# A two-layer decoder block on one core: the last group's softmax sums by ones on 32 columns, and another order for the last half's projection, layernorm and feed-forward

## The chip, the cores and the metric

One Trainium2 chip, one of its cores. The metric is the device time of one execution in microseconds, the median of several runs. The profile is one separate execution, with a time of its own.

## What is computed

Four sequences of 1024 tokens by 512 features go through a gated self-attention, a cross-attention to a context of 1024 by 384, and a small feed-forward, each after a layernorm and each added to its input. Everything is fp32. Cut to what the change touches (second attention and feed-forward):

```python
q = (layernorm(x) @ Wq + bq)          # 16 heads of 32
k, v = ctx @ Wk + bk, ctx @ Wv + bv
attn = softmax(q k^T / sqrt(32))      # 1024 x 1024 per head
x = x + (attn v) @ Wo + bo
s = layernorm(x) @ Win + bin_         # 512 -> 64
h = relu(s[..., None] * W1 + b1)      # 64 units, 16 hidden values each
x = x + ((h * W2).sum(-1) + b2) @ Wout + bout
```

## The kernel before, in words

`moderate_path` does the whole work; `general_path` follows only if a check of magnitudes (`marks`, then `flag`) fails. The order of every instruction is written out by hand. There are eight items `u`: phase 0 (self-attention) for four sequences, then phase 1 (cross-attention). An item has two halves `hf` of 512 queries, a half has four groups `g` of four heads, and a group has eight steps `kt`, one for each 128 keys.

A step (L659) computes the scores of four heads into two two-bank PSUM tiles `s` (L549), takes the exponential of each on ScalarE into `e` (L554; six buffers, so three steps' worth), and multiplies the previous step's `e` with the values into `av` (L576). The softmax sums are gathered in two ways. In items with `shared` set (phase 0 and the last item), VectorE adds up `e` of the first two heads over the steps (`es`, L562) and TensorE sums the other two by matmuls with a column of ones (`sm`, L584). In the other items VectorE adds up all four heads. When a group is done, `normalize` copies `av` and `sm` to SBUF, `add_up` (L603) sums `es` over partitions by ones, writes the sums to DRAM and reads them back spread over partitions; `divide` (L627) takes the reciprocals, writes these to DRAM and reads each head's row back to its 32 partitions (`recb`); `multiply` (L655) scales `av` into `q`, whose buffer is reused for the attention's output. These parts come steps later, by a list of due times (`after`, `apart`).

Other work is laid between the steps by `run`, which spreads a list of parts with loads over the 32 steps of a half; a `pause` is load without work. `beside` (L867) writes that list. For the last item it holds, for the half before: the projection (`o`, L705, two parts per tile of 128 tokens, with the residual and the statistics), layernorm (`ln`), the way through DRAM to transposed blocks (`xT`, `tr`), the first feed-forward matmul (`s`, L761). The hidden units (`h`, L776: one 128x256 activation on ScalarE and one accumulation `g` on VectorE each, sixteen times, with two buffers `hid`) and the last matmul (`out`, L794) of a half are held over to the next half.

After the last step (L937 to L957) comes the tail: the last `av`, the loads for the last half, the last group's sums through DRAM in three pieces (`soon.pop`) with the held hidden units between, the held outputs, and then the last half's own projection, layernorm, transposes on TensorE (`across`, L304), feed-forward and outputs, and the flag. There PSUM comes in single banks from `bank()`, of which there are two.

DMAs are issued by SP in the order written; each engine works through its own queue in order.

## Time and profile before

| what | value |
|---|---|
| median of 3 runs | 2274.4 us (2273.26 to 2275.88) |
| profiled execution: its time | 2271.7 us |
| its span | 2269.5 us |
| mean granted TensorE clock | 0.991 |
| TensorE busy | 2198.3 us (97%) |
| VectorE busy | 1566.7 us (69%) |
| ScalarE busy | 1237.1 us (55%) |
| last item's scores begin | about 1972 us |
| last exponential ends | 2198.19 us |
| last addition to the output ends | 2262.43 us |
| flag written | 2263.36 us |

Times in the profile count from the start of the span. Busy shares are averages over stages with different limits; the change lies in the last 300 us, so those are read by their own timeline and stretches. In a line of the timeline the first two numbers are start and duration, the bracket gives the idle time of the engine just before and what ended it. In a line of stretches, each engine's busy time and number of instructions are followed by the granted clock, the DMA engines' share and the GB/s they moved.

### The profile page before, as it was taken

The page shows a single profiled execution, that of the slowest core. Times are in us where ns is not written, and L with a number is a line of the kernel's source. Part 1 is how long each engine was busy: PE and PEld are TensorE (multiplying, and loading weights), DVE is VectorE, ACT ScalarE, POOL GpSimd, SP SyncE. Part 2 cuts the span into 40 slices and gives each one's busy share as a digit, 9 for nine tenths or more (in the row PEclk, how much of TensorE's full clock was granted, in tenths as well). Part 3 has the DMA queues.
Part 4 walks back from the last instruction along what each step waited for, and adds up shares of the span by engine and source line. Part 5 has one row for each costly group of instructions (what it writes and reads, how often), then busy time and mean ns, then how long its engine had stood idle before and what let it go on. Part 6 is the DMA issues. An engine that isn't in the chain of part 4 may idle for free.

```text
span 2269.5 us, 52806 instructions
## 1 busy us (share of the span) xinstructions
PE 2198.3 (97%) x22610; PEld 553.9 (24%) x22610; DVE 1566.7 (69%) x2478; ACT 1237.1 (55%) x1485; POOL 148.2 (7%) x146
## 2 busy tenths in 40 slices
PE   6999999999999999999999999999999999999985
PEld 2322222222222222222222222222222222222212
DVE  4469676796757957567685766777687877756555
ACT  0055545555455554555556565666657565667661
POOL 4000020000000000000000000101010100101011
PEclk9999999999999999999999999999999999999997
DMA  4421123021230211212312140313222132212131
GB/s 129 119 78 50 63 95 107 24 83 64 100 105 18 83 64 63 68 44 70 85 59 77 49 118 12 104 48 96 87 60 76 56 79 67 62 48 68 48 91 40
DMA packets 153861, 162.01 MB, mean 71 GB/s; under 512 B 46624, under 2 KB 92320, under 8 KB 152464
## 3 DMA queue, kind: packets, MB, share of 16 engines
q1 hardware_dynamic: 150160, 157.48, 23.1%
q8 instruction: 179, 2.93, 0.5%
q0 software_dynamic: 2144, 0.98, 0.3%
q14 instruction: 66, 0.54, 0.1%
q10 hardware_dynamic: 1312, 0.07, 0.0%
HBM read 115.68 MB, written 42.76 MB: 70 GB/s over the span
## 4 chain that ended last, share of the span: by engine, by line
PE 85%; DVE 6%; ACT 5%; DMA 2%; issue 2%; SPq 0%; DVEq 0%; ACTq 0%
PE f L87 33%; PE s L549 22%; PE av L576 19%; PE sm L584 6%; DVE es L562 4%; ACT e L554 3%; PE sm L606 3%; ACT hid L781 1%; PE f L798 1%; DMA w<-in_attn_Wo 1%; DVE g L787 1%; PE f L766 1%; DVE xT L302 0%; DMA sum_d<-both 0%; PE f L451 0%
## 5 line engine op out<-in xcount | busy, mean ns | idle before, releaser
L554 ACT ACTIVATE e<-s 128x1024 f32<-128x1024 f32 x1024 | 994.0, 1022 | 736.9 <-PE s L549 546.6
L562 DVE TENSOR_TENSOR es<-es,e 128x1024 f32<-128x1024 f32 x528 | 648.4, 1252 | 288.6 <-ACT e L554 287.9
L549 PE MATMUL s<-q,k 32*64 32x512 f32 x8192 | 631.1, 613 | 14.0 <-ACT e L554 12.3
L576 PE MATMUL av<-e,v 128*32 128x512 f32 x4096 | 553.2, 603 | 0.2 <-ACT e L554 0.2
L87 PE MATMUL f<-xT,w 128*32 128x512 f32 x2816 | 331.6, 592 | 0.0
L570 DVE SCALAR_TENSOR_TENSOR eg<-e,sw,eg 128x512 f32<-128x512 f32 x448 | 318.4, 746 | 2.3
L549 PEld LDWEIGHTS s<-q,k 32*64 32x64 f32 x8192 | 137.8, 129 | 477.0 <-ACT e L554 282.9
L87 PE MATMUL f<-w,q 128*32 128x512 f32 x2048 | 243.2, 596 | 0.2 <-DVE res L804 0.2
L560 DVE TENSOR_TENSOR es<-e 128x1024 f32<-128x1024 f32 x88 | 107.7, 1246 | 181.3 <-ACT e L554 175.6
L576 PEld LDWEIGHTS av<-e,v 128*32 128x32 f32 x4096 | 88.5, 108 | 404.0 <-issue 400.2
L87 PEld LDWEIGHTS f<-xT,w 128*32 128x32 f32 x2816 | 93.1, 110 | 210.4 <-issue 203.2
L584 PE MATMUL sm<-e,sw 128*2 128x512 f32 x1024 | 133.3, 592 | 0.0
L727 POOL TENSOR_TENSOR r<-res,bo_bc 128x512 f32<-128x512 f32 x32 | 40.9, 1278 | 1095.7 <-DVE res L719 725.5
L781 ACT ACTIVATE hid<-sT,units 128x256 f32<-128x256 f32 x128 | 74.8, 601 | 66.2 <-DVE sT L268 36.2
L87 PEld LDWEIGHTS f<-w,q 128*32 128x32 f32 x2048 | 67.0, 111 | 156.5 <-issue 149.9
L87 PE MATMUL f<-w,xT 128*32 128x512 f32 x896 | 104.6, 592 | 0.6 <-DVE q L268 0.6
L87 PE MATMUL f<-ctxT,w 128*32 128x512 f32 x768 | 92.3, 592 | 0.0
L87 PE MATMUL f<-w,ctxT 128*32 128x512 f32 x768 | 91.9, 592 | 0.0
L606 PE MATMUL sm<-es,ones 128*1 128x512 f32 x352 | 69.1, 591 | 4.2 <-DVE es L562 3.4
L787 DVE SCALAR_TENSOR_TENSOR g<-hid,units,g 128x256 f32<-128x256 f32 x120 | 57.9, 483 | 13.3 <-ACT hid L781 4.9
L719 DVE TENSOR_TENSOR res<-f,res 128x512 f32<-128x512 f32 x64 | 43.9, 686 | 30.6 <-PE f L87 30.6
L756 POOL TENSOR_TENSOR res<-res,bout_bc 128x512 f32<-128x512 f32 x28 | 59.8, 2143 | 66.0 <-DVE r L287 65.6
(240 smaller groups left out, 1060.1 us busy)
## 6 DMA issues: line engine op xcount, KB each, us to landing
recb<-rec_d SPq DMA_DIRECT2D x256, 64.0 KB
xT<-rows_d SPq DMA_DIRECT2D x60, 256.0 KB
rows_d<-r SPq DMA_DIRECT2D x60, 256.0 KB
w<-in_xattn_Wo SPq DMA_DIRECT2D x9, 1024.0 KB
xin<-in_x SPq DMA_DIRECT2D x8, 1024.0 KB
w<-wout_d SPq DMA_DIRECT2D x8, 1024.0 KB
res<-in_x SPq DMA_DIRECT2D x32, 256.0 KB
x1b_d<-r SPq DMA_DIRECT2D x32, 256.0 KB
```

Of the source, the lines that this page charges most:

```text
L87: nc.tensor.matmul(to[r], lhsT=lhsT[:, j, :] if len(lhsT.shape) == 3 else lhsT[:, r], rhs=rhs, **flags)
L549: nc.tensor.matmul(s[m : m + 64, j, :], lhsT=k[r, g, kt * P + m : kt * P + m + 64], rhs=q[r, g, :], start=True, stop=True,)
L554: nc.scalar.activation(e, s, AF.Exp, scale=SCALE)
L560: nc.vector.tensor_tensor(me["es"][i], me["e", 0][i], es[i], ALU.add)
L562: nc.vector.tensor_tensor(me["es"][i], me["es"][i], es[i], ALU.add)
L570: nc.vector.scalar_tensor_tensor(eg, es[0][:, h, :], gate(kt), eg, ALU.mult, ALU.add)
L576: nc.tensor.matmul(av[r, :], lhsT=me["v"][:, kt, HG * g + h, :], rhs=es[h // 2][:, h % 2, :], start=(kt == 0), stop=(kt == NT - 1),)
L584: nc.tensor.matmul(sm[j * DH : j * DH + sums, :], lhsT=me["sw"][:, t, HG * g + 2 + h, :] if ph == 0 else ones, rhs=me["e", t][1][:, h, :], ...
L606: nc.tensor.matmul(sm[j * DH : j * DH + 1, :], lhsT=ones, rhs=e, start=True, stop=True)
L756: return lambda: nc.gpsimd.tensor_tensor(res[t], res[t], bout_bc, ALU.add)
L781: nc.scalar.activation(hid, res["s"], AF.Relu, bias=units[:, 1, h : h + 1], scale=units[:, 0, h : h + 1])
L787: nc.vector.scalar_tensor_tensor(res["g"], res["hid"], units[:, 2, h - 1 : h], res["g"], ALU.mult, ALU.add)
```

## The change

The loop. In the last group of the last half (`closing`), VectorE adds up all four heads, TensorE's `sm` matmuls and `normalize` are left out. `beside` for the last item puts the weights and residuals first, spreads the first six held hidden units over pauses, lays the others between the projection's parts, puts the held outputs after the projection, and spreads the first eight of the new hidden units over the end of the half. The second half also fetches the tail's weights and residuals inside the loop.

The tail. `settle` multiplies each head's `es` with ones on 32 columns, so that the sums arrive on all 32 partitions of that head; reciprocal and product are taken for 128 tokens at a time, straight from PSUM. A tile's projection is split into chunks 0 to 2 and chunk 3, the only one that needs the last group. Tiles 2 and 3 project into the score banks (`behind`). Layernorm is done for two tiles at a time, with tiles 1 and 3 normalised on ScalarE; the output bias comes from a matmul with `share` (1/64) into the output's banks; inputs are computed for two tiles at a time; the flag stands ahead of most hidden units.

The diff, without a few renamings (`n`, `rs`):

```diff
@@ -105,6 +105,8 @@
         nc.gpsimd.memset(ones, 1.0)
+        share = const.tile([P, 1], F32, name="share")
+        nc.gpsimd.memset(share, 1.0 / M)
@@ -536,7 +539,12 @@
             shared = ph == 0 or u + 1 == len(order)
-            apart = 2 if u + 1 < len(order) else 3
+            def apart(g):
+                return 2 if u + 1 < len(order) else 3
+            def closing(g):
+                return (u, hf, g) == (len(order) - 1, 1, HG - 1)
@@ -554,7 +562,7 @@
                 me["e", kt] = es
-                for i in range(1 if shared else 2):
+                for i in range(1 if shared and not closing(g) else 2):
                     if kt == 1:
@@ -577,7 +585,7 @@
                     )
-                if shared and kt % 2:
+                if shared and kt % 2 and not closing(g):
@@ -622,7 +630,7 @@
                         )
-                after(apart, lambda: divide(g, i, both, c))
+                after(apart(g), lambda: divide(g, i, both, c))
@@ -650,7 +658,7 @@
                     )
-                after(apart, lambda: multiply(g, both, all_))
+                after(apart(g), lambda: multiply(g, both, all_))
@@ -669,7 +677,7 @@
                 times(g, kt, es)
-                if kt == NT - 1:
+                if kt == NT - 1 and not closing(g):
                     normalize(g)
@@ -677,6 +685,29 @@
+        def settle(u, hf, g):
+            me = S[u]
+            i = (u * 2 + hf) * HG + g
+            rec = p1.tile([P, HALF], F32, tag="recb", name="recb")
+            def sums():
+                for j in range(HG):
+                    nc.tensor.matmul(
+                        sm[j * DH : (j + 1) * DH, :], lhsT=ones.to_broadcast([P, DH]), rhs=me["es"][j // 2][:, j % 2, :],
+                        start=True, stop=True,
+                    )
+            def divide(t):
+                nc.vector.reciprocal(rec[:, ts(t, P)], sm[:, ts(t, P)])
+                nc.vector.tensor_tensor(me["q", hf][:, g, ts(t, P)], av[:, ts(t, P)], rec[:, ts(t, P)], ALU.mult)
+            def look():
+                nc.vector.tensor_reduce(marks[:, i : i + 1], sm, AX.X, ALU.add)
+                nc.vector.tensor_reduce(marks[:, NS + i : NS + i + 1], rec, AX.X, ALU.add)
+            return sums, divide, look
         def post(u, hf):
@@ -686,7 +717,7 @@
                 def f():
-                    if not last:
+                    if (u, hf) not in ((n - 2, 1), (n - 1, 1)):
                         r = res[t] = p4.tile([P, D], F32, tag="res", name="res")
@@ -703,11 +734,14 @@
             def project(t):
-                def part(cs):
+                def part(cs, to=None):
                     def f():
-                        assert me["divided", hf] == HG - 1
+                        assert me["divided", hf] >= cs[-1]
                         if cs[0] == 0:
-                            res["po"] = bank()
+                            res["po"] = to() if to else bank()
+                            res["po", t] = res["po"]
+                        if last:
+                            res["po"] = res["po", t]
                         for c in cs:
@@ -727,24 +761,43 @@
                     return len(cs), f
+                if last:
+                    return [part([0, 1, 2], behind if t > 1 else None), part([3])]
                 return [part([0, 1]), part([2, 3])]
-            def root():
+            def behind():
+                if not res.get("banks"):
+                    two = ps.tile([P, 2, HALF], F32, tag="s", name="s")
+                    res["banks"] = [two[:, i, :] for i in range(2)]
+                return res["banks"].pop(0)
+            def root(a=0, n=4):
                 if ph == 1:
-                    i = 2 * NS + b * NT + 4 * hf
-                    nc.gpsimd.tensor_copy(marks[:, i : i + 4], res["mv"][:, :, 1])
-                res["rs"] = rsqrt(res["mv"], 4)
+                    i = 2 * NS + b * NT + 4 * hf + a
+                    nc.gpsimd.tensor_copy(marks[:, i : i + n], res["mv"][:, a : a + n, 1])
+                rs = rsqrt(res["mv"][:, a : a + n, :], n)
+                for t in range(n):
+                    res["rs", a + t] = rs[:, t : t + 1]
+                if last:
+                    res["nm", a] = p2.tile([P, n], F32, tag="ve", name="nm")
+                    nc.vector.scalar_tensor_tensor(res["nm", a], res["mv"][:, a : a + n, 0], -1.0, rs, ALU.mult, ALU.mult)
...
                             res["xn"] = p1.tile([P, 4, D], F32, tag="tok", name="xn")
-                        normalized(res["xn"][:, t, :], res[t], res["mv"], res["rs"], t)
-                        nc.gpsimd.tensor_tensor(res[t], res[t], bout_bc, ALU.add)
+                        to = res["xn"][:, t, :]
+                        if t % 2:
+                            nc.scalar.activation(
+                                to, res[t], AF.Identity, bias=res["nm", t - 1][:, 1:2], scale=res["rs", t]
+                            )
+                        else:
+                            normalized(to, res[t], res["mv"], res["rs", t], t)
                         return
                     r2 = p2.tile([P, 1, D], F32, tag="r2", name="r2")
-                    normalized(r2[:, 0, :], res[t], res["mv"], res["rs"], t)
+                    normalized(r2[:, 0, :], res[t], res["mv"], res["rs", t], t)
                     away(rows_d[b][hf], r2, t, 1)
@@ -756,18 +809,25 @@
             def tr(t):
-                return lambda: (across if last else blocks)(res["xn"], t)
-            def inputs():
-                ss = bank()
+                def f():
+                    crossing[:] = [True] * (t != 2)
+                    across(res["xn"], t)
+                return f if last else lambda: blocks(res["xn"], t)
+            def inputs(ks=(0, 1)):
+                if 0 in ks:
+                    res["ss"] = bank()
+                ss = res["ss"]
                 for c in range(NC):
-                    for j in range(4):
+                    for j in range(2 * ks[0], 2 * ks[-1] + 2):
                         k, m = divmod(j, 2)
...
                         )
+                if 1 not in ks:
+                    return
                 sT = p2.tile([P, 2 * P], F32, tag="sT", name="sT", bufs=1)
@@ -793,11 +853,11 @@
                 def f():
-                    po = [bank(), bank()]
+                    po = res["bout", t] if last else [bank(), bank()]
                     for k in range(2):
...
                             po[k], lhsT=res["g"][k * M : (k + 1) * M, ts(t, P)], rhs=wout[k * M : (k + 1) * M, :],
-                            start=True, stop=True,
+                            start=not last, stop=True,
                         )
@@ -806,20 +866,32 @@
+            def bout(t):
+                def f():
+                    po = res["bout", t] = [behind(), behind()]
+                    for k in range(2):
+                        r = slice(k * M, (k + 1) * M)
+                        nc.tensor.matmul(
+                            po[k], lhsT=share[r].to_broadcast([M, P]), rhs=bout_bc[r, :], start=True, stop=False
+                        )
+                return f
             loads = [[(0, load(t)) for t in range(4)]]
...
                 "o": [project(t) for t in range(4)],
-                "ln": [[(0, root)]] + [norm(t) for t in range(4)],
+                "ln": ([[(0, lambda a=a: root(a, 2))] for a in (0, 2)] if last else [[(0, root)]])
+                + [norm(t) for t in range(4)],
             }
...
                 "xT": [] if last else [[(0, load_xT)]],
-                "b": [] if last else [[(0, biased(t))] for t in range(4)],
+                "b": [[(2, bout(t))] for t in range(2)] if last else [[(0, biased(t))] for t in range(4)],
                 "tr": [[(1 if last else 0, tr(t))] for t in range(4)],
-                "s": [[(2, inputs)]],
+                "s": [[(2, inputs)]] if not last else [[(1, lambda k=k: inputs((k,)))] for k in range(2)],
                 "h": [[(0, hidden(h))] for h in range(INNER + 1)],
@@ -869,13 +942,15 @@
             if u + 1 == n:
-                out = last["wo"] + end(pause(14)) + last["load"] + pause(2) + last["o"] + weave(last["ln"], pause(8))
-                out += last["xT"] + pause(10) + last["tr"] + weave(last["b"], pause(4)) + last["s"]
-                if hf == 0:
-                    out += pause(5)
-                else:
-                    out += weave(last["h"][0:6], pause(6))
-                    last["h"] = last["h"][6:]
+                h, out = held[0]["h"], last["wo"] + last["load"]
+                k = min(len(h), 6)
+                if hf:
+                    ending.append(post(u, 1))
+                    out += ending[0]["wo"]
+                out += weave(h[0:k], pause(12)) + weave(h[k:], last["o"]) + held.pop()["out"]
+                out += (ending[0]["load"] if hf else []) + weave(last["ln"], pause(5)) + last["xT"] + pause(8)
+                out += last["tr"] + weave(last["b"], pause(2)) + last["s"] + weave(last["h"][0:8], pause(14))
+                last["h"] = last["h"][8:]
                 held.append(last)
@@ -934,27 +1009,38 @@
                 run(attention(u, hf), beside(u, hf))
+        tail = ending[0]
+        sums, divide, look = settle(n - 1, 1, HG - 1)
         late.pop(0)()
-        crossing.clear()
-        tail, before = post(n - 1, 1), held.pop()
-        parts = lambda *names: sum((sum(tail[k], []) for k in names), [])
-        hidden = sum(before["h"], [])
-        run([lambda: None], [parts("wo", "load")])
-        soon.pop(0)[-1]()
-        run([lambda: None], [hidden[0:6]])
-        soon.pop(0)[-1]()
-        run([lambda: None], [hidden[6:]])
-        soon.pop(0)[-1]()
-        run([lambda: None], [sum(before["out"], []), parts("o", "ln", "xT", "b", "tr", "s", "h", "out")])
+        def go(*parts):
+            for _, f in parts:
+                f()
+        o, ln, b, tr, s = ([part for item in tail[k] for part in item] for k in ("o", "ln", "b", "tr", "s"))
+        h = [part for item in held[0]["h"] for part in item]
+        go(o[0])
+        sums()
+        go(o[2], *h[0:3])
+        for t in range(4):
+            divide(t)
+            go(*h[3 + 2 * t : 5 + 2 * t])
+        S[n - 1]["divided", 1] = HG - 1
+        go(o[1], o[3], *o[4:6], *sum(held[0]["out"], []), ln[0], *ln[2:4], *o[6:8], b[0], *tr[0:2], s[0])
+        go(ln[1], *ln[4:6], b[1], *tr[2:4], s[1])
+        look()
         fine = p1.tile([P, 2 * NS + B * NT], F32, name="fine")
...
         nc.tensor.matmul(pn[0:1, 0:1], lhsT=least, rhs=ones, start=True, stop=True)
+        h = sum(tail["h"], [])
+        go(*h[0:4])
         nc.vector.tensor_scalar(flag, pn[0:1, 0:1], P - 0.5, None, ALU.is_lt)
+        go(*h[4:], *sum(tail["out"], []))
```

More of the change, by code (lines that the diff above doesn't have):

```diff
@@ L286, in normalized @@
         def normalized(to, xt, mv, rs, i):
-            nc.vector.tensor_scalar(to, xt, mv[:, i, 0:1], rs[:, i : i + 1], ALU.subtract, ALU.mult)
+            nc.vector.tensor_scalar(to, xt, mv[:, i, 0:1], rs, ALU.subtract, ALU.mult)
         def away(rows, xt, t, n):
@@ L320, in moderate_path @@
         order = [(ph, b) for ph in range(2) for b in range(B)]
+        n = len(order)
         late = []
@@ L385, in f @@
                         xt = me["xn", hf][:, t, :]
-                        normalized(xt, xt, res["mv"], res["rs"], t)
+                        normalized(xt, xt, res["mv"], res["rs"][:, t : t + 1], t)
                         if xt0(hf):
@@ L859, in one @@
             return [[(0, f)]]
+        ending = []
         held = []
```

## The prediction

> **What bounds the kernel now.** I read the page first (busy shares, chain), then the timeline of the last batch item, the groups by shape, the stretches of the tail, and the chain in order of time.
>
> ```profile
> PE 2198.3 (97%) x22610; PEld 553.9 (24%) x22610; DVE 1566.7 (69%) x2478; ACT 1237.1 (55%) x1485; POOL 148.2 (7%) x146
> PE 85%; DVE 6%; ACT 5%; DMA 2%; issue 2%; SPq 0%; DVEq 0%; ACTq 0%
> ```
>
> TensorE bounds the whole. The change touches only the last item (u=7, from 1972 us) and what follows its attention, and there the limits are others. Timeline of that item (start, duration, engine, work, idle before):
>
> ```profile
> 2099.37 1.13 ACT L781 ACTIVATE hid<-sT,units 128x256 f32<-128x256 f32 x2 [0.35 <-DVE g L787]
> 2100.41 1.92 ACT L554 ACTIVATE e<-s 128x1024 f32<-128x1024 f32 x2
> 2101.46 2.00 PE L549 MATMUL s<-q,k 32*64 32x512 f32 x16
> ...
> 2157.15 1.11 PE L549 MATMUL s<-q,k 32*64 32x512 f32 x16
> 2159.38 2.00 PE L549 MATMUL s<-q,k 32*64 32x512 f32 x16
> ```
>
> A step's 16 score records take 1.06 us when both halves of the scores may be written, 2.00 when the second waits for the exponentials. The score starts 2157.15, 2163.17, 2169.19 give 6.02 us for two plain steps; 2011.84 to 2020.21 gives 8.37 for two with a projection part each (1.72), where TensorE is full; 2097.68 to 2104.72 gives 7.04 for two into which ScalarE has to fit five of the feed-forward's 128x256 activations.
>
> The tail, by stretches (us; busy time and count of PE, weight loads, DVE, ACT, POOL; clock; DMA):
>
> ```profile
> 2198.20:2216.49 18.29, 7.72 (x27) 1.92 (x25) 9.71 (x23) 8.44 (x15) 0.00 (x0) 0.72 0.14 45
> 2216.49:2232.20 15.71, 15.67 (x128) 4.09 (x128) 5.32 (x10) 0.00 (x0) 0.00 (x0) 0.89 0.10 35
> 2236.28:2245.50 9.22, 8.02 (x160) 5.90 (x160) 6.41 (x8) 0.00 (x0) 5.50 (x4) 0.81 0.01 2
> 2245.50:2256.04 10.54, 0.00 (x0) 0.00 (x1) 8.10 (x17) 9.36 (x16) 0.00 (x0) 0.75 0.00 1
> 2263.40:2269.50 6.10, 0.00 (x0) 0.00 (x0) 0.00 (x0) 0.00 (x0) 0.00 (x0) 0.50 0.16 51
> ```
>
> and as the chain has it:
>
> ```profile
> 2204.85 2.03 DMA cs<-sum_d
> ...
> 2210.18 1.99 DMA recb<-rec_d
> 2212.28 0.30 DVE q L656
> ...
> 2216.49 15.72 PE f L87 x128
> ...
> 2261.74 0.69 DVE res L804
> ```
>
> Call Z the end of the last exponential: 2198.19. Then nothing overlaps: the sums go through DRAM until Z+14.8, the held outputs until Z+18.3, the projection until Z+34.0, layernorm and transposes until sT at Z+47.3, hidden units until Z+57.9, the last addition at Z+64.2, the flag, the end at Z+71.3.
>
> **The change: the last item's steps.** Work in the loop is moved, not removed, but for 16 `sm` matmuls of the last group (4 x 0.86 = 3.4 us of PE).
>
> First half (1972.08 to 2083.51, 111.4 us). Steps 1-6 now carry one activation each. It fits ScalarE's wait of about 1.8 us in one step of a pair and costs some 0.2 over the 0.29 in the other: 3 pairs x 6.1, plus 0.3 for the copies of the first step, 18.6. Eight steps with a projection part, 4 x 8.37 plus 0.8 for the sums' matmuls between (2036.96 to 2041.53 is 4.57 against 3.76), 34.3; eleven activations lie in these steps' ScalarE waits (1.8 and 2.7 us in each pair). Two steps with outputs, 2 x (1.04+1.00+1.06)+0.86 = 7.1. Sixteen plain steps 48.2; the `win` matmuls, moved to the end of a group, 1.7 and activations again 0.7. Sum 110.6: gain 0.8.
>
> Second half (2083.51 to Z, 114.7). The same 18.8+34.3+7.1, then 24.1 for the third group. Last group: its first step with `win` 5.5 (as 2183.51 to 2189.03); then without `sm` a step is scores 1.06 and values 1.00, against ScalarE's 1.92+0.5: about 2.5 each, 19.0 to Z. Sum 108.8: gain 5.9. Both gains 6.7; from 3 (the activations hidden less well) to 9.
>
> VectorE pays: 14 additions of 1024 columns instead of 7, 1.15 each back to back (four in 4.62 at 1959.84), 7 `g` updates at 0.45, the third group's division and multiplication 1.4: 16.1+3.2+1.4 = 20.7 from the first exponential's end, 2.2 us into a group whose Z comes after 19.0. So the last addition ends near Z+3.6. Six `e` buffers, three steps, cover that lag; without them it would be ScalarE's.
>
> SP now issues the next weights (1 MB), residuals (1 MB) and in the second half another 1 MB at the half's start, ahead of the previous group's bounce. The DMAs moved 383 GB/s at 2194 to 2196, so 3 MB are 8 us; the division is asked for in the fifth step, 12 us in. Hidden; uncovered it would stop VectorE, then PE's first projection part.
>
> **The tail.** From Z on VectorE's order sets the pace; PE's first three projection chunks for two token tiles and the sums (o[0], o[2], 6 us) run beside it.
>
> - Additions end at Z+3.6; four `g` at 0.585 (16 activations in 9.36): Z+5.9. The sums on 32 columns, 1.04 as `sm` before, start at Z+3.6: hidden.
> - Four reciprocals 128x128, four products, six `g`. No such reciprocal is in the trace; two neighbours are:
>
> ```profile
> L643 DVE RECIPROCAL rec<-den 128x16 f32<-128x16 f32 x32 | 8.1, 253 | 1.1
> L477 DVE RECIPROCAL sw<-f 128x64 f32<-128x64 f32 x8 | 4.4, 550 | 0.0
> L787 DVE SCALAR_TENSOR_TENSOR g<-hid,units,g 128x256 f32<-128x256 f32 x120 | 57.9, 483 | 13.3 <-ACT hid L781 4.9
> ```
>
> 48 columns cost 0.297, 6.2 ns each; 128 give 0.95. [...] The second neighbour reads PSUM as well: I take 0.95. Product 0.29 by the same copies, gaps 0.04: 4 x 1.32 + 6 x 0.57 = 8.7, Z+14.6. This takes the place of 4.5+4.8 us of bounce.
> - Three tiles' addition, statistics, aggregate (0.73+0.73+0.20): Z+19.6; PE has them ready from Z+8 to Z+14. Four held outputs, 2.8 and 1.6 of waiting for banks (as 2214.2 to 2215.7): Z+23.9. The root for two tiles is as long as for four, 2.4, and `nm` 0.2; a normalisation 0.55 (1.02 before, with POOL beside it): Z+27.0.
> - Fourth tile: PE starts it when the held outputs have left, Z+21.7. Its 3.44 us become 5.2, since the clock was 0.50 from 2216.5 to 2220 after a like pause: Z+27.1. Then 1.7+2.6+0.55: Z+31.9.
> - Its transposes, 1.1, copy 0.75, 1.1, copy 0.65, half the inputs 1.2: sT at Z+36.7 (before Z+47.3).
> - Hidden units as before, 10.5: Z+47.2. All four output matmuls at once, 2.1 and 1.8, then two additions, 1.4: Z+52.5; the bias is in PSUM, the two bias pairs hidden in PE's waits; the check of `marks` lies before the hidden units.
> - The end came 6.1 us after the flag, 7.1 after the last addition; I take 6.5: Z+59.0.
>
> Gain 71.3-59.0 = 12.3. [...] After Z+14 PE has only short bursts. [...]
>
> Sum: 6.7+12.3 = 19.0. Span 2269.5 to 2250.5; that execution's time 2271.7 to 2252.7; the median of the runs stands 2.7 above it, so 2255.4.
>
> **Rivals.**
> 1. As worked out: 2255.4, own range 2250 to 2260; chance 0.70.
> 2. The loop gives nothing: the spread activations and VectorE's doubled additions hold up the exponentials as much as the clumps did. For it: an activation waits for the `g` two before, now queued behind long additions. Against: 1.8 us of ScalarE wait. Tail alone: 2262.1; 0.14.
> 3. [...] 2261.4; 0.10.
> 4. Slower: the bounce of the previous half's last group, behind the 3 MB. PE, in order, stands at the projection part of each half's eighth step until the product is there. The steps leave 9 us to each leg where 4.5 and 4.8 were needed. To eat 19 us, and 4.5 for a visible loss, both halves' bounces must be some 12 us later than their slots, transfers at a third of the rate seen. 2280; 0.03.
> 5. It does nothing: PE waits for all four products before any projection, and the loop gains nothing. Against: the first three chunks read none of them, and 8.6 us of idle PE before L798 are there to be filled. 2274; 0.03.
>
> **The numbers.** Below 2250 only if the loop gives 9 and the clock holds. 2249 to 2262.5 leaves out rivals 4 and 5 and some of each edge of the others, about 0.2. Measurement tells about 0.2%, 4.5 us: faster 0.94, same 0.03, slower 0.03.
>
> **What would show it.** Projection matmuls right after the last `av`, no DMA between sums and product; score starts 6.0 to 6.2 apart for pairs in steps 1-6 of both halves; Z near 2191.5; the last addition to `es` 3 to 4 us after Z; reciprocals of 0.95; sT at Z+37; the last addition at Z+52. Wrong: a DMA stall of VectorE in the first eight steps, reciprocals over 1.2, a fourth tile projected after Z+30.

## The result

The changed kernel takes 2256.25 us, median of 4 runs (2255.34 to 2258.3), the kernel before 2275.14 in the runs beside them: a ratio of 0.9915, 95% interval 0.9903 to 0.9928, or 18.9 us less (16.4 to 22.1). A second measurement gave 2253.74 and 0.9906 (0.9891 to 0.9921). The profiled execution took 2255.34, its span 2253.5. Forecast were 2255.4 and 19.0 us.

From the page of the changed kernel, busy time by engine (with its share of the span) and the shares of the chain that ended last:

```profile
PE 2192.8 (97%) x22590; PEld 552.6 (25%) x22590; DVE 1572.1 (70%) x2498; ACT 1238.2 (55%) x1488; POOL 142.9 (6%) x144
PE 84%; DVE 7%; ACT 4%; DMA 2%; issue 2%; SPq 0%; DVEq 0%; ACTq 0%
```

As before, the whole says nothing of the change; it lies in the last item and behind. Its timeline, in the first steps of the first half and the last two before Z, the end of the last exponential (now 2194.14):

```profile
1986.54 1.34 PE L557 MATMUL s<-q,k 32*64 32x512 f32 x16
1986.62 0.60 ACT L841 ACTIVATE hid<-sT,units 128x256 f32<-128x256 f32 x1
...
1987.69 1.94 ACT L562 ACTIVATE e<-s 128x1024 f32<-128x1024 f32 x2 [0.47 <-PE s L557]
...
1988.80 1.97 PE L557 MATMUL s<-q,k 32*64 32x512 f32 x16
...
1989.52 0.60 ACT L841 ACTIVATE hid<-sT,units 128x256 f32<-128x256 f32 x1
...
2188.40 1.39 PE L557 MATMUL s<-q,k 32*64 32x512 f32 x16
...
2189.05 0.60 ACT L841 ACTIVATE hid<-sT,units 128x256 f32<-128x256 f32 x1 [0.40 <-DVE g L847]
2189.56 1.94 ACT L562 ACTIVATE e<-s 128x1024 f32<-128x1024 f32 x2
...
2190.72 1.92 PE L557 MATMUL s<-q,k 32*64 32x512 f32 x16
```

One activation stands in each step, and ScalarE still waits (0.47) in every second one of the first steps. In the last group, exponential plus activation, 1.94 + 0.60 and short gaps, make up the step of 2.64 on average. From the item's first score to Z it takes 216.49 us where it took 226.11.

The tail in stretches (columns as before: busy time and count of PE, weight loads, DVE, ACT, POOL; clock; DMA):

```profile
2194.14:2207.08 12.94, 12.27 (x110) 4.38 (x108) 12.14 (x23) 5.30 (x10) 0.00 (x0) 1.00 0.00 1
2207.08:2215.00 7.92, 5.14 (x16) 1.47 (x16) 6.26 (x13) 0.00 (x0) 0.19 (x1) 0.86 0.18 66
2222.80:2225.90 3.10, 3.04 (x24) 1.27 (x28) 1.00 (x5) 0.83 (x2) 0.00 (x0) 1.00 0.00 0
2231.60:2242.20 10.60, 0.00 (x0) 0.00 (x0) 7.72 (x17) 9.70 (x17) 0.00 (x0) 0.74 0.01 2
2242.20:2246.20 4.00, 3.79 (x8) 1.19 (x8) 1.41 (x4) 0.00 (x0) 0.00 (x0) 0.50 0.09 30
2247.40:2253.50 6.10, 0.00 (x0) 0.00 (x0) 0.00 (x0) 0.00 (x0) 0.00 (x0) 0.50 0.26 94
```

In the first stretch TensorE and VectorE are now both nearly full, 12.27 and 12.14 of 12.94 us; in the stretch of the bounce before, they were busy for 7.72 and 9.71 of 18.29. The chain in order of time (start, duration, what) shows who set the end, VectorE up to the held outputs and TensorE from there to sT (the copy that the tail's hidden units start from):

```profile
2203.71 0.88 DVE recb L702
...
2211.58 0.68 DVE res L864
...
2214.98 4.18 PE s L87 x32
2219.16 1.06 PE s L875 x4
...
2222.86 1.92 PE f L824 x16
2224.79 1.06 PE s L875 x4
```

The tail from Z takes 59.36 where it took 71.31. So the parts that the change touches gave 9.62 + 11.95 = 21.6 us in the profiles, where the medians have 18.9 (16.4 to 22.1). The difference is the start, which the change doesn't touch: this execution began its last item at 1977.65, that of before at 1972.08. These 5.6 us arose at three places. The first scores came at 113.3 instead of 111.1. One step of the second group took 1.8 longer, on a clock of 0.80 instead of 1.00 (first line before, second changed):

```profile
166.16:173.08 6.92, 5.68 (x52) 1.30 (x48) 6.85 (x11) 2.96 (x3) 0.00 (x0) 1.00 0.14 38
168.30:177.02 8.72, 7.32 (x53) 1.47 (x49) 8.65 (x14) 2.96 (x3) 0.00 (x0) 0.80 0.11 30
```

One step of the 47th group took 1.7 longer, by just as much as VectorE waited longer for the DMA of `recb` (7.94 instead of 6.22):

```profile
1647.14 0.69 DVE L656 TENSOR_TENSOR q<-both,recb 128x512 f32<-128x512 f32 x1 [6.22 <-DMA recb<-rec_d]
1652.72 0.69 DVE L664 TENSOR_TENSOR q<-both,recb 128x512 f32<-128x512 f32 x1 [7.94 <-DMA recb<-rec_d]
```

Everything else together comes to 0.1 us. The other profiles differ at the same places and at one more, the third step of the first item, near 118 us: 5.50 at a clock of 1.00 in these two, 8.3 to 8.6 at 0.59 to 0.60 in seven others. In all fourteen profiles of this study the last item starts between 1972.08 and 1981.20, and the one of before is the earliest: it had a clock of 1.00 in both steps and the shortest wait for that DMA. So what follows compares parts: the item's first score to Z, and Z to the end. The medians carry a spread that no edit made.

### The profile page after: what moved, and what is told of

It reads as the page before. It is cut to its first block, busy times and chain, and to the rows that moved or that the text cites. A ratio compares the mean times of both kernels' runs of the same rounds, so it can differ in the third digit from the quotient of the medians.

```text
span 2253.5 us, 52768 instructions
## 1 busy us (share of the span) xinstructions
PE 2192.8 (97%) x22590; PEld 552.6 (25%) x22590; DVE 1572.1 (70%) x2498; ACT 1238.2 (55%) x1488; POOL 142.9 (6%) x144
## 4 chain that ended last, share of the span: by engine, by line
PE 84%; DVE 7%; ACT 4%; DMA 2%; issue 2%; SPq 0%; DVEq 0%; ACTq 0%
PE f L87 32%; PE s L557 22%; PE av L584 18%; PE sm L592 6%; DVE es L570 4%; ACT e L562 3%; PE sm L614 3%; DVE g L847 1%; DMA w<-in_attn_Wo 1%; ACT hid L841 1%; PE f L858 1%; PE f L824 1%; DMA rec_d<-rec 0%; DVE xT L304 0%; DMA wae<-in_attn_Wa 0%
## 5 line engine op out<-in xcount | busy, mean ns | idle before, releaser
L87 PE MATMUL f<-w,q 128*32 128x512 f32 x1984 | 238.1, 592 | 0.7 <-DVE q L703 0.7
L664 DVE TENSOR_TENSOR q<-both,recb 128x512 f32<-128x512 f32 x63 | 46.3, 735 | 27.9 <-DMA recb<-rec_d 27.8
```

What stands on the lines that cost most here:

```text
L87: nc.tensor.matmul(to[r], lhsT=lhsT[:, j, :] if len(lhsT.shape) == 3 else lhsT[:, r], rhs=rhs, **flags)
```

## The experiments

The table has, in us, the last item's first score to Z, the tail behind Z, their sum, and where several rounds ran the median and the ratio to before with its interval. A ratio is to the runs of before beside that kernel, whose median was 2274.0 to 2275.7, so it is not the quotient of the medians shown. A row without one is a single execution.

| kernel | loop | tail | sum | median | ratio |
|---|---|---|---|---|---|
| before | 226.11 | 71.31 | 297.42 | 2275.14 | |
| changed | 216.49 | 59.36 | 275.85 | 2256.25 | 0.9915 (0.9903 to 0.9928) |
| changed, again | 216.50 | 59.15 | 275.65 | 2253.74 | 0.9906 (0.9891 to 0.9921) |
| new list alone | 218.72 | 71.71 | 290.43 | 2270.42 | 0.9964 (0.9950 to 0.9978) |
| new tail, old list | 225.84 | 60.06 | 285.90 | 2266.32 | 0.9946 (0.9929 to 0.9964) |
| ones on 32 columns alone | 226.99 | 72.67 | 299.66 | 2276.84 | 1.0001 (0.9989 to 1.0013) |
| changed, bounce back | 218.72 | 64.90 | 283.62 | 2264.20 | 0.9936 (0.9911 to 0.9960) |
| late bias pairs | 216.50 | 58.76 | 275.26 | | |
| the same, five idle matmuls | 216.50 | 57.70 | 274.20 | | |
| fewer additions | 216.18 | 58.74 | 274.92 | | |
| whole tiles | 216.66 | 60.43 | 277.09 | | |
| held additions off VectorE | 216.84 | 56.22 | 273.06 | | |
| four tiles first | 216.52 | 59.55 | 276.07 | 2255.58 | 0.9921 (0.9908 to 0.9935) |
| all three edits | 216.52 | 54.67 | 271.19 | 2251.80 | 0.9887 (0.9869 to 0.9904) |

### Which part brings what

**The new list alone** (the `else` of the old list goes with it):

```diff
-                out = last["wo"] + end(pause(14)) + last["load"] + pause(2) + last["o"] + weave(last["ln"], pause(8))
+                h, out = held[0]["h"], last["wo"] + last["load"]
+                k = min(len(h), 6)
+                out += weave(h[0:k], pause(12)) + weave(h[k:], last["o"]) + held.pop()["out"]
+                out += weave(last["ln"], pause(5)) + last["xT"] + pause(8)
...
```

> The kernel before with one part of the change alone: the new list of work beside the last item's two halves (activations spread over the first steps, projection parts from the seventh step on, residuals loaded early). The last group still takes 16 sm matmuls and the bounce, and the tail is the old one. Theory (the list itself helps, as read from the two traces): steps 1 to 6 of each half shrink as in the changed kernel, so from the item's first score to Z 2.9 + 6.7 us less, minus some 2.3 for the last group that keeps its sm matmuls: 7 to 8 us less than 226.1, tail 71 as before, median 7 us lower. Rival (the gain in the loop comes from the last group and from the shift at the start, the list gives nothing): 226 to Z, median within 3 us of before.

Loop 7.4 us shorter, tail as before: the theory. The median is 5.3 lower than that of before beside it, where 7 was expected. The rival, that the list gives nothing, is out: the ratio's interval (5 to 11 us) excludes the 3 us that it allowed.

**The new tail with the old list:**

```diff
-                h, out = held[0]["h"], last["wo"] + last["load"]
+                out = last["wo"] + end(pause(14)) + last["load"] + pause(2) + last["o"] + weave(last["ln"], pause(8))
...
+                    out += weave(last["h"][0:6], pause(6))
```

> The changed kernel with the old list of work beside the last item, so the tail and the last group are new and the loop is old. Theory: tail 59.4 as in the changed kernel (12 us below before), last group 24.4 (2.3 below), the rest of the loop as before; median 14 us below before, 5 us above the changed kernel; the two experiments together then give back the whole. Rival (list and tail depend on each other: with the old list the hidden units and held outputs come at another time and the tail grows): tail of 62 us or more.

The tail is what was expected within 0.7, so the rival is out; in the two parts the gain is 11.5, not 14. But the last group did not get 2.3 us shorter by losing its `sm` matmuls: 26.48, against 26.77 before and 24.43 in the changed kernel. Up to its last step it had gained 2.6, and the last step gave 2.3 of that back: 5.4 us where it took 3.1 before. The timeline there shows why:

```profile
2194.61 1.91 PE L824 MATMUL f<-xn,win 128*32 128x256 f32 x32
...
2199.43 1.09 ACT L841 ACTIVATE hid<-sT,units 128x256 f32<-128x256 f32 x2
...
2201.77 2.35 DVE L570 TENSOR_TENSOR es<-es,e 128x1024 f32<-128x1024 f32 x2
...
2204.04 1.07 DVE L847 SCALAR_TENSOR_TENSOR g<-hid,units,g 128x256 f32<-128x256 f32 x2
2204.61 0.60 ACT L841 ACTIVATE hid<-sT,units 128x256 f32<-128x256 f32 x1 [1.78 <-DVE g L847]
```

In the old list the activations come in a clump in the last three steps. With two buffers `hid`, the fourth has to wait for `g`, and `g` stands on VectorE behind the additions to `es`, which the change has doubled. ScalarE stands for 1.78, and the last exponential, next in its queue, with it. That is the mechanism of the prediction's second rival, an activation behind long additions, and in the old order of work it is there. In the new list the activations are spread evenly, and these waits are 0.2 to 0.4. (The line of TensorE is for later: the inputs whole, 32 records in 1.91.) In the new list with `sm` kept the same group takes 26.65: there TensorE fills it, busy for 26.3. Either edit alone gives 0.1 to 0.3, both give 2.3. So 7.4 + 0.3 fall short of the 9.6 of the loop by just this.

**Ones on 32 columns alone**, the rest of the tail in the old order:

```diff
-                for i in range(1 if shared else 2):
+                for i in range(1 if shared and not closing(g) else 2):
...
-        soon.pop(0)[-1]()
-        run([lambda: None], [hidden[0:6]])
...
+        sums()
+        run([lambda: None], [hidden[0:3]])
+        for t in range(4):
+            divide(t)
+            run([lambda: None], [hidden[3 + 2 * t : 5 + 2 * t]])
```

> The kernel before with only the last group's sums changed: no sm matmuls in it, both es buffers filled by VectorE, the sums on 32 columns, reciprocal and product in four pieces, no DMA; all of the tail behind it in the old order (the projection starts when all four products are there, the flag last). Theory: the loop 2.3 us shorter in the last group; the products end at Z + 13 to 14.5 where the bounce ended at Z + 14.8, so alone the new division brings at most 2 us in the tail: median 2 to 5 us lower, nearly all of it from the loop. Rival (the bounce was what cost, and its removal is most of the tail's 12 us): median 10 us or more lower.

Less than the theory allowed: nothing at all, the interval being 0.9989 to 1.0013. The products are complete at Z + 12.0 instead of Z + 14.8, but `g`, which finished during the bounce, now alternates with the reciprocals on VectorE until Z + 13.0; the old order has the held outputs next, and those end at Z + 19.4 (18.9 before). The last group keeps 26.5 for the reason just told. And 1.2 of this execution's loop is another matter, a stretch in the second half's third and fourth step where the clock fell in full work:

```profile
2098.72:2100.40 1.68, 1.68 (x12) 0.36 (x12) 0.76 (x2) 1.68 (x3) 0.00 (x0) 0.52 0.07 17
2100.40:2102.30 1.90, 1.90 (x17) 0.20 (x9) 1.77 (x3) 1.55 (x3) 0.00 (x0) 0.53 0.07 7
```

Without that it is some 1.1 us worse than before in these parts, all in the tail. That is partly the held outputs' 0.5 and partly a clock of 0.69 instead of 0.81 under the transposes; the rest was not followed further.

**The changed kernel with the bounce back:**

```diff
-                return (u, hf, g) == (len(order) - 1, 1, HG - 1)
+                return False
...
-        sums()
-        go(o[2], *h[0:3])
-        for t in range(4):
-            divide(t)
-            go(*h[3 + 2 * t : 5 + 2 * t])
+        soon.pop(0)[-1]()
+        go(o[2], *h[0:3])
+        soon.pop(0)[-1]()
+        go(*h[3:])
+        soon.pop(0)[-1]()
```

> The changed kernel with the old division of the last group: 16 sm matmuls, the sums through DRAM, three stages; the new order of projection, layernorm and feed-forward stays. Theory: last group 2.3 us longer; the products at Z + 14.8 instead of Z + 12.9, and with VectorE free during the bounce the held outputs can't go earlier, as they stand behind the products in its order: tail 2 us longer. Median 4 to 5 us above the changed kernel. Rival (VectorE's additions in the last group are the price of the new division, so the old one costs less than the sum): 0 to 2 us above. Rival (the bounce collides with the early residual and weight loads): 8 us or more above.

The loop is the 2.2 longer, the tail 5.5 instead of 2. The step missed: the bounce hands over all 512 columns at once, and TensorE stands until then.

```profile
2214.30 0.69 DVE L664 TENSOR_TENSOR q<-both,recb 128x512 f32<-128x512 f32 x1 [1.38 <-DMA recb<-rec_d]
2215.05 1.93 PE L87 MATMUL f<-w,q 128*32 128x512 f32 x8 [8.73 <-DVE q L664]
```

In the changed kernel the first tile's last chunk runs after a quarter of the division (Z + 6.4), and the third tile is projected at Z + 13.1, just as VectorE gets free of the divisions (Z + 12.9). With the bounce they come after Z + 15.8, at a clock of 0.50 after 8.73 us of standing (8 records in 1.93 where they took 1.07), and the third tile's statistics end at Z + 25.2 instead of 17.5. So the same division is worth 7.8 us in loop and tail of the new order and nothing in the old.

### What sets the tail's pace

**Fewer additions:**

```diff
-                for i in range(1 if shared and not closing(g) else 2):
+                for i in range(1 if (shared and not closing(g)) or (closing(g) and 1 < kt < 7) else 2):
```

> The changed kernel without five of the seven additions to the second es in the last group (key tiles 2 to 6): so it leaves out part of the sums of two of the four heads, and with them 5 x 1.18 = 5.9 us of VectorE. Theory (VectorE is 3.0 us behind at Z, and its order sets the tail's pace): additions end near Z + 1.2, the first reciprocal starts at Z + 3.3 instead of Z + 5.1, and everything to the end comes 1.8 us earlier, Z + 57.6; in the loop the last group stays at 24.4, as ScalarE sets it. Rival (TensorE sets the pace from the projection on): first reciprocal earlier, end within 0.5 of Z + 59.4. Rival (VectorE holds up ScalarE in the last group): group of 22.5 or less.

Nearest to the first rival, just outside its 0.5: the first reciprocal starts at Z + 4.6 (3.3 by the theory), the end comes 0.6 us earlier. The last group is 0.3 shorter, so the second rival (22.5 or less) is out. With its lag gone, VectorE waits for the sums instead:

```profile
2196.95 0.96 DVE L702 RECIPROCAL recb<-sm 128x128 f32<-128x128 f32 x1 [0.91 <-PE sm L696]
```

TensorE takes the sums after `o[0]` and among the first of `o[2]`, up to Z + 4.5; the lag of 3 us costs less than 1, since TensorE's own work covers the rest.

**Whole tiles:** the last group's chunk first in each tile, no chunk ahead of its product.

```diff
-        go(o[0])
         sums()
-        go(o[2], *h[0:3])
+        go(*h[0:3])
...
-                        for c in cs:
+                        for k in cs:
+                            c = (k + 3) % NC if (u, hf) == (n - 1, 1) else k
```

> The changed kernel with the tail's projection taken tile by tile, the last group's chunk first, so that no projection matmul runs before the product of its own tile. Times from Z. Theory (VectorE's order sets the pace; TensorE has slack of 5 us and more): the first tile's 3.44 us start after the first product, Z + 6.4, at half clock for a while, so the three tiles are ready near Z + 11.5, 15 and 18.5 where VectorE asks for them at 12.9, 14.4 and 15.9: its three additions end 1.5 to 2.5 later, and the end comes at Z + 60.5 to 62. Rival (the early chunks are what the tail's gain comes from): the end at Z + 65 or later.

Three tiles at Z + 20.4 instead of 17.5, the end 1.07 later: the theory's end, from a delay of 2.9 where it said 1.5 to 2.5. Part comes back because TensorE, busy until then, did the fourth tile in 3.64 where the changed kernel took 4.25. The early chunks are worth 1 us, not the gain.

**Late bias pairs:**

```diff
-        go(..., *o[6:8], b[0], *tr[0:2], s[0])
-        go(ln[1], *ln[4:6], b[1], *tr[2:4], s[1])
+        go(..., *o[6:8], *tr[0:2], s[0])
+        go(ln[1], *ln[4:6], *tr[2:4], s[1])
...
-        go(*h[0:4])
+        go(b[0], b[1], *h[0:4])
```

> The changed kernel with both bias pairs issued behind the check of marks, among the tail's hidden units, instead of ahead of the transposes. Times are from Z, the end of the last exponential, in the profile. Theory (the second pair stands on TensorE's path between the first half of the inputs and the transposes of the third tile, 1.06 us, and the first pair pushes the transposes of the first tile by 0.99, and with them the first half of the inputs): sT at Z + 35.6 instead of Z + 37.4, end at Z + 57.5 instead of Z + 59.4. Rival (VectorE's second root sets the transposes of the third tile, the pairs are hidden as forecast): end within 0.3 of Z + 59.4.

The end came 0.6 earlier, between the two forecasts, but in this execution the fourth tile's projection, ahead of every edit, took 5.47 instead of 4.25:

```profile
2214.11 5.47 PE L87 MATMUL s<-w,q 128*32 128x512 f32 x32
...
2219.40 1.92 PE L311 MATMUL f<-ident,xn 128*32 128x128 f32 x64
```

From the end of that projection to the end of the span it is 32.52 where the changed kernel has 34.34: 1.82 less, as the theory had it. The pairs were on the path.

**The same with five idle matmuls:**

```diff
         go(b[0], b[1], *h[0:4])
+        for _ in range(5):
+            nc.tensor.matmul(av, lhsT=ident, rhs=bout_bc, start=True, stop=True)
```

> As the run with the late bias pairs, and five 128x512 matmuls more that nobody reads, written into the spent av bank while ScalarE and VectorE work on the tail's hidden units; they add work and take none away. They are to keep TensorE busy, 8 us or so of the 10.7, up to the output matmuls, which took 2.18 us to the first pair at a granted clock of 0.50. Theory (the idle stretch halves the clock, and a busy one restores it): the first pair in 1.1 us, the four additions without a gap, end 1.1 to 1.5 us earlier than with the late pairs alone. Rival (the clock stays down for short work, or the matmuls come to stand ahead of the outputs): 0, or up to 1 us later.

The end came 1.06 earlier than with the late pairs alone, near the forecast, but by luck: 0.86 of it is the fourth tile's projection (4.61 instead of 5.47), ahead of the edit. From sT on it is 0.2, not the 1.1 to 1.5. The five took 4.56 us, not 8, and left TensorE idle for 4.35 before the outputs, which ran at a clock of 0.57 (2.18 to the first pair). Ten were tried later.

**Held additions off VectorE:**

```diff
-                        nc.vector.tensor_tensor(res[i], po[k], res[i], ALU.add)
+                        if (u, hf) == (n - 1, 0):
+                            r2 = p2.tile([P, D], F32, tag="r2", name="r2")
+                            nc.scalar.copy(r2, po[k])
+                            nc.gpsimd.tensor_tensor(res[i], r2, res[i], ALU.add)
+                        else:
+                            nc.vector.tensor_tensor(res[i], po[k], res[i], ALU.add)
```

> The changed kernel with the four additions of the held outputs taken off VectorE in the tail: ScalarE copies them out of PSUM, GpSimd adds. Theory (VectorE's order sets the pace; these additions and their waits take 4.1 us of it between the third tile and the first root): first root at Z + 17.5 instead of Z + 21.6; but the fourth tile's projection still has to follow the output matmuls and its banks, so norm(2) moves less, 1.5 to 3 us, and the end to between Z + 56.4 and Z + 57.9. Rival (GpSimd's additions slow VectorE's small operations beside them, as the normalisation with GpSimd beside it took 1.02 against 0.54): less than 1 us, or later.

3.1 us earlier, as the theory had it at best. The rival's mechanism is there as well, but not its end, less than 1 us. The timeline at the root:

```profile
2214.32 3.80 POOL L867 TENSOR_TENSOR res<-r,res 128x512 f32<-128x512 f32 x3 [0.23 <-ACT r L866]
...
2214.72 0.91 DVE L276 TENSOR_SCALAR ve<-fmv 128x2 f32<-128x2 f32 x1
...
2215.28 3.64 PE L87 MATMUL s<-w,q 128*32 128x512 f32 x32
...
2215.65 1.23 DVE L278 TENSOR_SCALAR yi<-ve 128x2 int32<-128x2 int32 x1
...
2216.92 1.22 DVE L279 TENSOR_SCALAR yi<-yi 128x2 int32<-128x2 int32 x1
...
2218.17 0.16 DVE L283 SCALAR_TENSOR_TENSOR nw<-yi 128x2 f32<-128x2 f32 x1
```

Three operations on two columns, 0.17 each elsewhere, take 0.91 to 1.23 beside GpSimd's additions of 1.27 each, and 0.16 again once those are done: 2.9 us lost. Each of the three took 0.7 to 1.0 times as long as one such addition; why was not shown. What is gained in spite of it: the root starts 4.1 earlier, and the fourth tile follows at once on a clock of 1.00.

### Versions meant to beat it

**Four tiles first:**

```diff
-        go(o[1], o[3], *o[4:6], *sum(held[0]["out"], []), ln[0], *ln[2:4], *o[6:8], b[0], *tr[0:2], s[0])
-        go(ln[1], *ln[4:6], b[1], *tr[2:4], s[1])
+        go(o[1], o[3], *o[4:8], *sum(held[0]["out"], []), *ln)
+        go(*sum(held[0]["held"], []), *tr[0:2], s[0], *tr[2:4], s[1])
...
+        for _ in range(10):
```

> A version meant to beat the changed kernel: in the tail all four tiles are projected and added before the held outputs, one root serves all four; the held outputs are copied out of PSUM by ScalarE and added by VectorE after the normalisations; both bias pairs and ten 128x512 matmuls that nobody reads stand among the hidden units, the latter for the clock. Expected from Z: VectorE's four tiles end at Z + 19.0, root and nm at Z + 21.6, norm(2) at Z + 22.8 (29.8 in the changed kernel), then transposes and inputs in 9 us: sT at Z + 31.5 (37.4), first output pair at full clock, end at Z + 52 (59.4), 7 us less than the changed kernel. Rival (TensorE, cold again before the transposes, or the held outputs' banks hold up the transposes): sT at Z + 34 or later, gain of 4 us or less.

No gain: sT at Z + 38.6. The rival's side, by a wait that neither named:

```profile
2203.77 3.62 PE L87 MATMUL s<-w,q 128*32 128x512 f32 x32
2210.87 5.33 PE L87 MATMUL s<-w,q 128*32 128x512 f32 x32 [3.48 <-DVE res L753]
```

The fourth tile's bank is the second half of one two-bank tile whose first half the third tile uses; its matmuls waited until VectorE had read the third tile's sum (Z + 16.6), stood 3.5 us and then took 5.33 instead of the third tile's 3.62, the clock being down to 0.51. That a bank of its own would cure it was not tried. The cold transposes that the rival named came too: 64 records in 3.62 at a clock of 0.53, where the changed kernel took 1.95 at 1.00. Ten matmuls that nobody reads worked, though: from the last `g` to the end 10.3 us instead of 11.3.

The changed kernel ran once more beside it:

> The changed kernel once more, timed beside the version above, on the same chip and against the same runs of before. Theory (the run-to-run spread lies in the start, up to some 8 us, and at one place near 1,680 us; the rest repeats to 0.01 us): loop of 216.5 and tail of 59.4 again, with the tail off by up to 1.2 where the clock stands otherwise at the fourth tile's projection; median 17 to 22 us below before.

216.50 and 59.15, and 20.3 us below before: as expected.

**All three edits:** held additions off VectorE, late bias pairs, ten idle matmuls.

> The changed kernel with three edits that earlier runs priced one by one: the held outputs copied by ScalarE and added by GpSimd (tail 56.2 instead of 59.4), both bias pairs behind the check of marks (in that run the second pair still stood 1.06 us on the path), and ten unread 128x512 matmuls among the hidden units (in the version with four tiles first, from the last g update to the end 10.3 us instead of 11.3). Theory (the three add up): sT at Z + 33.7, end at Z + 54.1, 5 us below the changed kernel, 26 below before in the profile's own parts and about 24 in the medians. Rival (the clock's phase takes a part back, or the pieces cover the same wait): end between Z + 55.5 and Z + 56.5.

They add up: tail 54.67 against 54.1 expected (sT at Z + 33.9, last `g` to the end 10.5). The four additions at the end run without a gap:

```profile
2241.66 2.48 DVE L869 TENSOR_TENSOR res<-s,res 128x512 f32<-128x512 f32 x4 [1.45 <-PE s L858]
```

In the parts that is 4.5 to 4.7 us better than the changed kernel; the ratio to before is 0.9887 (0.9869 to 0.9904). That interval overlaps the changed kernel's own, and the two were not run side by side, so by the medians alone the order of the two is likely, not certain.

## Why the prediction was right, and where it was not

The forecast time and the two timed measurements of the changed kernel agree within 2 us, the mechanism is the forecast one, and the rivals are out: the loop's gain is 9.6 and not nothing, the tail's 11.95 and not half of the 12.3 forecast, and no fourth tile is projected after Z + 30 (it ends at Z + 25.0). Of the DMA stall that would have spoken for the fourth rival there is one small one: VectorE waits 1.19 us for `recb` in the first half's sixth step, and neither TensorE nor ScalarE waits for it. But the number is better than its parts, and that is luck. They gave 21.6 where 19.0 was forecast, and the sum was made against an execution of before that reached the last item 2.8 to 9.1 us earlier than any other profiled one; the 2.7 added for the median corrected a part of that.

- **First half, forecast gain 0.8, measured 2.9.** The first six steps took 17.1 instead of 18.6: the three pairs 5.99, 5.16 and 5.98 where 6.1 was set, so the activation, said to cost 0.2 in the second step of a pair, costs nothing. The steps with projection parts took 35.2 instead of 34.3, the outputs 7.05 instead of 7.1, the sixteen plain steps with the `win` matmuls 49.1 instead of 50.6. The list alone (7.4 over both halves) shows that the gain is the list's.
- **Second half, forecast 5.9, measured 6.7.** The last group's 24.43 was forecast as 24.5, with the right sum (ScalarE's 1.92 + 0.6 a step). What the working gave as the reason, the `sm` matmuls taken away, is half of it: without the activations spread evenly ScalarE waits 1.78 for `g` in the last step, and the group keeps 26.5. So the wait that the second rival named is real; what kept it out of the changed kernel is the new list.
- **VectorE to norm(0), forecast Z + 27.0, measured Z + 24.5.** The reciprocal took 0.951 us, as worked out from its two neighbours' rows. The product took 0.29, as worked out from copies of before, 0.689 at 512 columns and 0.424 at 256 (L268). Additions to `es` ended at Z + 3.0 instead of 3.6, the four divisions with six `g` between them took 7.8 instead of 8.7, and the held outputs 4.2 of the 4.3 forecast.
- **norm(2) and sT: two errors that cancel.** norm(2) ended at Z + 29.8, 2.1 earlier than forecast, but from there to sT it took 7.6 us instead of 4.8, for the next two reasons. So sT came at Z + 37.4, forecast Z + 36.7, and the end at Z + 59.4, forecast Z + 59.0. That these agree is luck.
- **"The two bias pairs hidden in PE's waits": wrong.** From the fourth tile on TensorE's only waits were of 0.75 to 0.9 us, behind the copies of the transposes, and the pairs did not stand in them. One pair pushed the transposes, the other stood between the inputs and the third tile's transposes; putting both later gave 1.8.
- **"Half the inputs 1.2": 1.92, twice.** The clock was 1.00 in that stretch, so it isn't the clock. Whole, 32 records over four groups of 32 columns take 1.91; each half has two groups, and its 16 take as long. Splitting them by token pairs saved no time on the array, and cost 0.7 for each half against the forecast.
- **The clock.** In the transposes' stretch of before it was 0.81; now the transposes ran at 1.00, 64 records in 1.95 and 32 in 1.08, the 64 right behind 5.2 us of matmuls. The third rival's 2261.4 held 3 us for a lower clock, an estimate that no run shows: with four tiles first, where a wait stood ahead of them, 64 records took 3.62 at 0.53, 1.7 more. The output matmuls, costed at 2.1 and 1.8, took 3.79 at 0.50 (8 records, behind 10.76 in which TensorE did nothing); with ten unread matmuls before them they took 1.99 at 1.00. The fourth tile's projection, forecast at 5.2, took 4.25; in kernels with the same order up to that point it took 4.25, 4.31, 4.35, 4.61, 4.85 and 5.47.
- **The division's worth.** The forecast set reciprocals in place of the bounce's legs, 8.7 against 9.3 us, and left the rest to the order. That they hand over a quarter at a time is what TensorE lives on, and it is 5.5 of the tail's 12 us; in the old order it is nothing.

The start is executions differing, not the change: the new list alone and the 32-column ones alone, which have the code of before ahead of the last item, reach it at 1976.07 and 1977.74. The 47th group's step is 0.6 to 1.9 us longer in every other profile than in that of before, each time by as much as VectorE waited longer for `recb`. What stays open is why that DMA came later, and why the clock differed in the two early steps.

## What to carry to other kernels

Two limits of nearly the same size hide each other: taking matmuls off TensorE put additions on VectorE, and these held up ScalarE wherever its work came in a clump; spreading that work left TensorE as the limit. Each gave 0.1 to 0.3 us alone, both gave 2.3; so price an edit in the order of work that it will stand in. Handing a result over in pieces is worth something only if the consumer's order can start on a piece. And work parked "in an engine's waits" must be put where the chain, not the busy share, shows such waits after the change.

## What the runs showed of the hardware

- Identical code ahead of the change ended between 1972.1 and 1981.2 us in fourteen profiles; all of it but some 0.2 arose ahead of the first scores, in two steps where the granted clock lay between 0.59 and 1.00 (near 118 and 166 us), and in one where VectorE waited 6.2 to 8.1 us for a DMA (near 1655 us). The 1400 us between repeated to about 0.1 us.
- The same 32 projection records took from 4.25 to 5.47 us after a stretch in which TensorE was busy for about two thirds of the time (5.14 of 7.92 us in the changed kernel), and 3.64 where other matmuls ran right before. What made these runs differ from each other was not shown.
- Once, in one profile, the granted clock fell to 0.52 for 3.6 us in the middle of the loop, at a cost of 1.2 us; the only idle time of TensorE just ahead was 0.94.
- Matmuls on two of the four groups of 32 columns took as long as twice as many on all four: 16 in 1.92, 32 in 1.91.
- ScalarE, in order, stood 1.78 us at an activation whose buffer was not free, with the last exponential behind it.
- VectorE operations on two columns took about as long as the GpSimd addition beside them (1.27), 0.91 to 1.23 us instead of 0.17.
